# A state-space image block: the work between two batches' scans is rewritten (channels as 128 + 64, means summed on GpSimd, convolution in halves, a new order)

## The chip, the cores and the metric

The kernel runs on one core of a Trainium2 chip. The core has five engines, each with its own instruction queue: TensorE (PE, matrix products into PSUM), VectorE (DVE), ScalarE (ACT), GpSimd (POOL) and SyncE (SP, which here issues all DMAs). Engines meet only through semaphores. The metric is the device time of one launch in microseconds (us).

## The reference

The input x is 8 images of 64 x 64 positions with 192 channels, in float32. Two layers are applied, each as x + layer(groupnorm(x)). The change is in layer 1 (and in where layer 0's constants live), whose core is this:

```python
xz = jnp.einsum('bhwc,dc->bhwd', x, in_proj_w)          # 192 -> 768
xc, z = jnp.split(xz, 2, axis=-1)                       # 384 + 384 channels
xc = depthwise 3x3 convolution of xc; xc = silu(xc + conv_b)
xs = [rows, columns, rows reversed, columns reversed]   # K = 4 walks over 4096 positions
# per walk: x_dbl = x_proj(xs) -> dts, B, C;  delta = softplus(dt_proj(dts) + bias)
hst = exp(delta * A) * hst + (delta * u) * B            # 16 states a channel, 4096 steps
y   = sum over states of hst * C
y   = sum of the four walks (with + xs * Ds)
y   = layernorm(y) * ln_gamma + ln_beta
y   = y * silu(z)
out = einsum('bhwd,cd->bhwc', y, out_proj_w)            # 384 -> 192
```

## The kernel before

**Layer 0** works on all images first and leaves its result x1 in DRAM, channels outermost: 192 rows of 4,096 positions. Its means over channels use GpSimd adds (`s`, line 362) and one product with a matrix of ones.

**Layer 1** goes image by image ("batch" b). A batch has three parts:

- *front*: project x1 to the 384 channels of xc, fill a padded image, convolve, Silu, store to DRAM in row order and, turned, in column order (`xo`).
- *scan*: 32 steps (4 walks of 8 tiles), each with 24 units of states and channels. Per unit ScalarE makes the decays `ea`, PE turns the weighted inputs into `g`, VectorE runs `tensor_tensor_scan` (line 1596), GpSimd multiplies by C (`hc`, line 1610) and PE sums the states (`y`, line 1625). Results are added up in `yacc`, which stays in SBUF: 128 partitions x 3 groups of channels x 4,096 positions.
- *finish*: layer norm over the 384 channels of `yacc`, gate by silu(z), output projection, residual add, store.

The last loop of `layer1` runs for b = 0 to 8. In iteration b the finish of batch b-1 and the front of batch b are interleaved, together with the scan's prologue (the first chunk's loads, projections and weights); then the scan of batch b follows. So there are one front alone, seven boundaries (finish and front together) and one finish alone.

**How a boundary is ordered.** Front, finish and prologue are generators that yield `step(engine, weight, do)`, `"wait"` and `"take"` (a slot of a pool). `Flow` is a list planner: it keeps an estimated time per engine, picks the step that could start first (with `RANK` times the chain's rank as a bias), and fixes the instructions of each engine in that order. At run time every engine works through its list strictly in order. Weights, `LAG` and ranks only influence the order.

**The pieces.** Channels of x1 lie as 2 groups of 96 on 96 partitions (`CP, CT = 96, 2`). The front projects each tile of 512 positions with two products of 96 rows (`project`, line 1139), ScalarE copies the result into the pad (line 1169). When all eight tiles of a group of 128 channels are in, ScalarE does tap 0 (line 1190) and VectorE eight taps over 4,096 positions each (line 1200: `xs = pad * weight + xs`, three groups). Silu (line 1213) is done in halves, then a copy in turned order (line 1227) and the stores (1218, 1230). In the finish the mean is three products of `yacc` with a matrix of 1/384 (`mean`, line 1247), then VectorE subtracts (1255), ScalarE squares (1265), a second mean gives the variance, ScalarE makes 1/sqrt by Ln and Exp (1283, 1284), VectorE multiplies (1290), ScalarE applies gamma and beta (1297). The gate projects x1 again (1327), Silu (1345), VectorE multiplies (1357), PE projects back to 2 x 96 channels (1374), VectorE adds x1 (1383), SP stores (1386). The prologue loads `xc` and `wd` (1428, 1431), makes `p_d`, `xdbl`, `p_dt`, the softplus `spa`, `de`, `du` on GpSimd (1489), `duT`, and ten weightings `pw` (1554) before the first scan. In PSUM five banks (`mm`) serve all this, two the front's projection (`fx`), one the scan's prologue in steady state.

Of the kernel before, what the change touches and what calls it, by code (L numbers as in the profile page):

```python
# [16 lines left out]
CP, CT = 96, 2  # L17
# [73 lines left out]
class Flow:  # L91
# [48 lines left out]
    def start(self, req, ready):  # L140

        if req[0] == "wait":
            return (-1.0, max(ready, self.at[req[1]])) if req[1] in self.at else None
        if req[0] == "take":
            return (-1.0, max(ready, min(self.slots[req[1]]))) if self.slots[req[1]] else None
        engine, _, _, after, table = req
        t = max(ready if after is None else after, self.free[engine])
        if engine == "ACT" and table and table != self.table:
            return t + self.TABLE + self.STAY, t + self.TABLE
        return t, t  # L150

    def run(self):
        while self.chains:
# [8 lines left out]
            if req[0] == "take":  # L162
                self.slots[req[1]].remove(min(self.slots[req[1]]))
# [866 lines left out]
def layer1(tc, consts, x1s, mv1, out, w_in, w_x, w_dt, w_out):  # L1030
    nc = tc.nc
    ident, low, up, grp, eps, ones96, ones1, p96, p128 = consts
# [3 lines left out]
    image = lambda ap: ap.rearrange("(t p) l -> p t l", p=CP)  # L1036

    with ExitStack() as ctx:
# [8 lines left out]
        wi = wp.tile([CP, CT, 2 * DIN], F32, name="wi1")  # L1047
        nc.sync.dma_start(out=wi, in_=w_in.rearrange("(t p) m -> p t m", p=CP))
# [25 lines left out]
        sc, sh = gn_affine(tc, sp, mp, mv1.rearrange("p b t s -> p (b t) s"), grp, eps)  # L1074
        pb = mp.tile([128, TT], F32, name="p_gb", tag="mm")
        for m in range(2 * DT):
            for ct in range(CT):
                nc.tensor.matmul(
                    pb[:, m * nb : m * nb + nb],
                    wi[:, ct, m * 128 : m * 128 + 128],  # L1080
                    sh.rearrange("p (b t) -> p b t", t=CT)[:, :, ct],
                    start=ct == 0,
                    stop=ct == 1,
                )
# [3 lines left out]
        wxz = [wp.tile([CP, CT, DIN], F32, name=f"wi1{n}") for n in "xz"]  # L1088
# [4 lines left out]
        def scaled(f, b, half):  # L1093

            for ct in range(CT):
# [5 lines left out]
                            wxz[half][:, ct],  # L1101
                            wi[:, ct, half * DIN : half * DIN + DIN],
                            AF.Copy,
                            scale=sc[:, b * CT + ct : b * CT + ct + 1],
# [5 lines left out]
        def front(f, cx, mq, b, xo):  # L1110
# [3 lines left out]
            for tag, n in (("xl", 3), ("fx", 2), ("pad", 2), ("xs", 2), ("xt", 1)):  # L1114
                f.pool(tag, n)
            got = {}

            def load():
                for d in range(DT):
                    for t in range(NT):  # L1120
                        tk = slice(t * TT, t * TT + TT)
                        yield "take", "xl"
                        xl = got["xl", d, t] = fp.tile([CP, CT, TT], F32, name="xl1", bufs=3)
                        r = yield step("SP", 0.1, lambda: [nc.sync.dma_start(out=xl, in_=image(x1s[b])[:, :, tk])])
                        f.at["xl", d, t] = r + 3

            def project():
                yield from scaled(f, b, 0)
                for d in range(DT):
                    for t in range(NT):  # L1130
                        yield "wait", ("xl", d, t)
                        xl = got["xl", d, t]
                        yield "take", "fx"
                        ps = got["ps", d, t] = mq.tile([128, TT], F32, name="p_x1", tag="fx", bufs=2)
                        r = f.at["ps", d, t] = yield step(
                            "PE",
                            1.9,
                            lambda: [
                                nc.tensor.matmul(
                                    ps, wxz[0][:, ct, d * 128 : d * 128 + 128], xl[:, ct], start=ct == 0, stop=ct == 1  # L1140
                                )
                                for ct in range(CT)
                            ],
                        )
                        f.give("xl", r)

            def fill():
# [11 lines left out]
                for d in range(DT):  # L1159
# [18 lines left out]
                    f.at["pad", d] = r  # L1178

            def convolve():  # L1180
                for d in range(DT):
                    yield "wait", ("pad", d)
                    yield "take", "xs"
                    xs = got["xs", d] = fp.tile([128, HI, WI], F32, name="xs1", bufs=2)
                    tap = lambda j: pads[d % 2][:, j // 3 : j // 3 + HI, j % 3 : j % 3 + WI]
                    r = yield step(
                        "ACT",
                        3.7,
                        lambda: [
                            nc.scalar.activation(  # L1190
                                xs, tap(0), AF.Identity, bias=v["kb"][:, d : d + 1], scale=kw[:, d, 0:1]
                            )
                        ],
                    )
                    for j in range(1, 9):
                        r = yield step(
                            "DVE",
                            4.4,
                            lambda: [
                                nc.vector.scalar_tensor_tensor(xs, tap(j), kw[:, d, j : j + 1], xs, ALU.mult, ALU.add)  # L1200
                            ],
                            r - f.LAG,
                        )
                    f.give("pad", r)
                    f.at["conv", d] = r

            def store():
                for d in range(DT):
                    yield "wait", ("conv", d)
                    xs = got["xs", d]  # L1210
                    for h in range(2):
                        half = xs[:, h * HI // 2 : h * HI // 2 + HI // 2]
                        r = yield step("ACT", 1.9, lambda: [nc.scalar.activation(half, half, AF.Silu)], None, "silu")
                        r = yield step(
# [5 lines left out]
                                    in_=half.rearrange("p h w -> p (h w)"),  # L1220
                                )
                            ],
                            r,
                        )
                    yield "take", "xt"
                    xt = fp.tile([128, WI, HI], F32, name="xt1")
                    r = yield step("ACT", 7.2, lambda: [nc.scalar.copy(xt, xs.rearrange("p h w -> p w h"))])
                    f.give("xs", r + 5)
# [4 lines left out]
                f.at["front"] = r  # L1233

            return [convolve(), fill(), project(), load(), store()]

        def finish(f, cx, mq, b):
# [3 lines left out]
            for tag, n in (("sq", 1), ("rs", 2), ("z", 2), ("xl2", 3)):  # L1241
# [4 lines left out]
            def mean(ps, src):  # L1246
                return [nc.tensor.matmul(ps, on, src[:, d], start=d == 0, stop=d == DT - 1) for d in range(DT)]

            def centre():
                for t in range(NT):  # L1250
                    yv = yacc[:, :, tk(t)]
                    yield "take", "mm"
                    pm = mq.tile([128, TT], F32, name="p_m", tag="mm")
                    q = yield step("PE", 2.8, lambda: mean(pm, yv), 0.0)
# [4 lines left out]
            def square():  # L1259
                for t in range(NT):  # L1260
# [5 lines left out]
                    yield "take", "mm"  # L1266
                    pv = got["pv", t] = mq.tile([128, TT], F32, name="p_v", tag="mm")
                    r = yield step("PE", 2.8, lambda: mean(pv, sq))
# [39 lines left out]
            def load():  # L1308
                for t in range(NT):
                    yield "take", "xl2"  # L1310
                    xl = got["xl2", t] = fp.tile([CP, CT, TT], F32, name="xl2", bufs=3)
                    r = yield step("SP", 0.1, lambda: [nc.sync.dma_start(out=xl, in_=image(x1s[b])[:, :, tk(t)])])
                    f.at["xl2", t] = r + 3

            def gate():
                yield from scaled(f, b, 1)
                for t in range(NT):
                    yield "wait", ("xl2", t)
                    xl = got["xl2", t]
                    for d in range(DT):  # L1320
                        yield "take", "mm"
                        ps = got["pz", t, d] = mq.tile([128, TT], F32, name="p_z1", tag="mm")
                        f.at["pz", t, d] = yield step(
                            "PE",
                            1.9,
                            lambda: [
                                nc.tensor.matmul(
                                    ps, wxz[1][:, ct, d * 128 : d * 128 + 128], xl[:, ct], start=ct == 0, stop=ct == 1
                                )
                                for ct in range(CT)  # L1330
                            ],
                            f.at["xl2", t],
                        )

            def silu():
                for t in range(NT):
                    yield "take", "z"
                    z = got["z", t] = fp.tile(full, F32, name="z", bufs=2)
                    for d in range(DT):
                        yield "wait", ("pz", t, d)  # L1340
                        ps = got["pz", t, d]
                        p = yield step(
                            "ACT",
                            0.6,
                            lambda: [nc.scalar.activation(z[:, d], ps, AF.Silu, bias=gb[:, DT + d, b : b + 1])],
                            None,
                            "silu",
# [507 lines left out]
```

## Time and profile before

| what | us |
|---|---|
| three runs: lowest, median, highest | 24181.09, 24186.39, 24191.97 |
| the profiled execution: its time | 24176.65 |
| the profiled execution: span from the first to the last instruction | 24174.9 |
| layer 0 and first front, up to the first scan | 5049.5 |
| one batch, scan to scan | 2,404 |
| of that: between the last scan of a batch and the first of the next | 237.8 to 240.1 |
| last scan to the end | 137.0 |

Times in the profile count from the first instruction's start. A row of a group gives line, engine, operation, tiles (output <- inputs), shape and count; then busy time and mean duration in ns; then the idle time of the engine just ahead of these instructions and what ended it. A row of the timeline has start, duration (several merged instructions: from the first's start to the last's end), engine, line, operation, tiles and count. "PEld" is the load of weights into PE; each float32 product shows as two passes. A row of a stretch has the busy time and count of each engine, then PE's granted clock, the busy share of the DMA engines and GB/s.

### The profile page before, as it was taken

How to read it: one execution, taken by the hardware profiler on the slowest of the kernel's cores; microseconds unless marked ns; L12 is line 12 of the kernel's file. 1: busy time of each engine (PE TensorE's matmuls, PEld its weight loads, DVE VectorE, ACT ScalarE, POOL GpSimd, SP SyncE). 2: the span in 40 equal slices, each digit the busy share in tenths (PEclk: the TensorE clock that was granted, in tenths of full speed). 3: DMA queues.
4: the chain of work that ended last, by engine and by line, in shares of the span. 5: the costliest groups of instructions: out<-in, count | busy, mean ns of one | idle time of the engine just before them, and what ended most of it. 6: DMA issues, size and time to landing. Idle time of an engine off the chain costs nothing.

```text
span 24174.9 us, 313055 instructions
## 1 busy us (share of the span) xinstructions
PE 20986.5 (87%) x100036; PEld 10182.8 (42%) x100036; DVE 21386.3 (88%) x22093; ACT 21415.5 (89%) x38076; POOL 16907.4 (70%) x13639
## 2 busy tenths in 40 slices
PE   7999999978888888888888888888888888888888
PEld 4444444434443444344434443444344434443444
DVE  7888888779998998899889988998899989998998
ACT  5666766679998999899989998999899989998998
POOL 1111111159986998699869986998699779977997
PEclk8999999989999999999999999999999999999999
DMA  2111111122222222222222222222222222222222
GB/s 49 44 44 44 49 44 42 36 86 67 68 66 87 68 67 68 89 66 66 69 87 68 68 68 86 67 68 70 84 68 67 76 78 67 68 75 82 67 67 58
DMA packets 1129702, 1608.05 MB, mean 67 GB/s; under 512 B 259360, under 2 KB 458432, under 8 KB 1118848
## 3 DMA queue, kind: packets, MB, share of 16 engines
q1 hardware_dynamic: 1128064, 1588.03, 23.4%
q8 instruction: 806, 13.21, 0.2%
q14 instruction: 832, 6.82, 0.1%
HBM read 1024.65 MB, written 160.17 MB: 49 GB/s over the span
## 4 chain that ended last, share of the span: by engine, by line
POOL 53%; PE 25%; issue 8%; DVE 6%; ACT 5%; DMA 2%; SPq 1%; POOLq 0%; DVEq 0%; ACTq 0%
POOL hc L1610 47%; POOL cy L1608 4%; PE y L1625 3%; PE p_f L953 3%; DVE xs L1200 3%; PE p_f L973 2%; PE p_x L445 2%; PE g L1580 2%; ACT pw L1554 2%; DMA xc<-xo 2%; PE p_o L870 1%; POOL du L1489 1%; ACT ea L1569 1%; PE p_y L787 1%; PE p_d L1439 1%
## 5 line engine op out<-in xcount | busy, mean ns | idle before, releaser
L1610 POOL TENSOR_TENSOR hc<-hs,cb 128x1024 f32<-128x1024 f32 x6144 | 14577.7, 2373 | 10.3 <-POOL cy L1608 6.7
L1596 DVE TENSOR_TENSOR_SCAN hs<-ea,cy,g 128x512 f32<-128x512 f32 x10752 | 13069.7, 1263 | 783.2 <-PE g L1580 468.3
L1554 ACT ACTIVATE pw<-duT,bt 128x384 f32<-128x384 f32 x16384 | 8875.8, 601 | 11.6 <-DVE duT L1502 11.6
L1625 PE MATMUL y<-hc,sel 128*64 128x512 f32 x24576 | 6658.3, 620 | 2229.1 <-POOL hc L1610 2221.3
L1569 ACT ACTIVATE ea<-dr,an 128x512 f32<-128x512 f32 x12288 | 8123.2, 709 | 159.9 <-DVE hs L1596 131.9
L1580 PEld LDWEIGHTS g<-ident,pw 128*128 128x128 f32 x49152 | 5309.6, 141 | 4320.1 <-issue 2676.5
L1580 PE MATMUL g<-ident,pw 128*128 128x128 f32 x49152 | 6793.2, 280 | 32.4 <-DVE hs L1596 12.9
L1625 PEld LDWEIGHTS y<-hc,sel 128*64 128x64 f32 x24576 | 1229.6, 135 | 3648.1 <-POOL hc L1610 3385.1
L1489 POOL TENSOR_TENSOR du<-de,xc 128x512 f32<-128x512 f32 x768 | 982.9, 1280 | 1632.9 <-DVE de L1482 1618.2
L1608 POOL COPY cy<-hs 128x2 f32<-128x2 f32 x6144 | 1161.7, 189 | 1324.4 <-DVE hs L1596 1211.9
L1596 DVE TENSOR_TENSOR_SCAN hs<-ea,g 128x512 f32<-128x512 f32 x1536 | 1777.0, 1204 | 178.7 <-PE g L1580 138.3
L362 POOL TENSOR_TENSOR s<-xs 96x512 f32<-96x512 f32 x64 | 121.0, 1891 | 2033.2 <-DVE xs L340 1522.3
L1200 DVE SCALAR_TENSOR_TENSOR xs<-pad,p,xs 128x4096 f32<-128x4096 f32 x192 | 860.8, 4484 | 37.6 <-ACT xs L1190 30.4
L1468 PE MATMUL p_dt<-xdbl,wd 13*128 13x512 f32 x1536 | 856.8, 639 | 41.7 <-DVE de L1482 39.7
L362 POOL TENSOR_TENSOR s<-sq 96x512 f32<-96x512 f32 x128 | 210.3, 1643 | 961.7 <-ACT sq L375 890.7
L1439 PE MATMUL p_d<-xc,wx 128*44 128x512 f32 x1536 | 792.2, 598 | 95.0 <-DMA xc<-xo 95.0
L340 DVE SCALAR_TENSOR_TENSOR x<-xx,p,x 96x512 f32<-96x512 f32 x1024 | 784.4, 814 | 19.4 <-ACT x L329 19.4
L953 PE MATMUL p_f<-h,wf 96*128 96x512 f32 x1536 | 764.1, 633 | 24.4 <-ACT zs L547 14.0
L340 DVE SCALAR_TENSOR_TENSOR xs<-xin,p,xs 96x512 f32<-96x512 f32 x1024 | 749.5, 768 | 4.6 <-ACT xs L329 4.6
L1482 DVE SCALAR_TENSOR_TENSOR de<-p_dt,spa 128x512 f32<-128x512 f32 x768 | 524.1, 682 | 254.0 <-ACT spa L1477 253.0
L973 PE MATMUL p_f<-m,wf 128*96 128x512 f32 x1536 | 693.3, 602 | 0.0
L1495 PEld LDWEIGHTS p_du<-ident,du 128*128 128x128 f32 x3072 | 323.1, 141 | 743.2 <-POOL du L1489 500.3
(201 smaller groups left out, 19729.0 us busy)
## 6 DMA issues: line engine op xcount, KB each, us to landing
cb<-cd SPq DMA_DIRECT2D x4096, 128.0 KB
dr<-de SPq DMA_DIRECT2D x3072, 128.0 KB
xc<-xo SPq DMA_DIRECT2D x256, 768.0 KB
e<-csd SPq DMA_DIRECT2D x256, 384.0 KB
xl<-x SPq DMA_DIRECT2D x256, 384.0 KB
xo<-xs SPq DMA_DIRECT2D x48, 1024.0 KB
xo<-xt SPq DMA_DIRECT2D x24, 2048.0 KB
xl<-in_x SPq DMA_DIRECT2D x64, 384.0 KB
```

The costliest lines, as they stand in the source:

```text
L340: nc.vector.scalar_tensor_tensor(im(out[:, ct]), tap(ct, j), w[:, ct, j : j + 1], im(out[:, ct]), ALU.mult, ALU.add)
L953: nc.tensor.matmul(ps, wf1[:, ct, mt * 128 : mt * 128 + 128], h[:, ct], start=ct == 0, stop=ct == 1)
L973: nc.tensor.matmul(ps[:CP], wf2[:, kt, ct * CP : ct * CP + CP], m[:, kt], start=kt == 0, stop=kt == 5)
L1200: nc.vector.scalar_tensor_tensor(xs, tap(j), kw[:, d, j : j + 1], xs, ALU.mult, ALU.add)
L1489: o(nc.gpsimd.tensor_mul(st["du", d], st["de", d], st["xc"][:, d]))
L1554: nc.scalar.activation(st["pw", p, j][:, :, i], st["duT"][:, j].rearrange("p (g c) -> p g c", c=64), AF.Copy, scale=st["bt"][:, j, n : n + 1],
L1569: nc.scalar.activation(ea[:, f], state[s]["dr", d][:, f], AF.Exp, scale=an[:, k, p, at : at + 1])
L1580: nc.tensor.transpose(g[:, f, j * 128 : j * 128 + 128], state[s]["pw", p, j][:, 2 * d + f].rearrange("p a b -> p (a b)"), ident,)
L1596: nc.vector.tensor_tensor_scan(rev(h[:, f]), rev(ea[:, f]), rev(g[:, f]), 0.0 if first(s) else state[s - 1]["cy"][:, p, d, f : f + 1], ALU ...
L1608: o(nc.gpsimd.tensor_copy(st["cy"][:, p, d], h[:, :, last]))
L1610: o(nc.gpsimd.tensor_mul(hc, h, bc(st["cb", p], 1, [128, 2, TT])))
L1625: o(nc.tensor.matmul(y[half[f]], sel, hc[:, f], start=p == 0 and k > 0, stop=p == NP1 - 1))
```

## The change

In layer 1's front and finish only; the scan's code is the same.

- **Channels as 128 + 64.** x1, `wi` and the scaled weights lie as 128 channels on 128 partitions, and the other 64 of two neighbouring tiles side by side: tile t on partitions 0 to 63, tile t+1 on 64 to 127 (`parts`). A pair of tiles is loaded by three DMAs and projected by four products (`pair`): two of 128 rows, and two of 64 rows on different halves of the array. The output projection makes 128 channels per tile and the 64 of both tiles side by side in one PSUM tile; residual adds go from four of 96 partitions a pair to three of 128. The group norm's scale and shift go through DRAM once to lie the same way (`affd`, `aff`).
- **Means** first add the three channel groups on GpSimd (two adds of 128 x 512), then one product.
- **Convolution in halves** of 32 rows: tap 0 and the taps of a half start when its part of the pad is filled, Silu, store and turned copy follow by halves.
- **Order anew**: every chain has a rank, `RANK` is 1.0, `LAG` 0.35, new weights; `take` can ask for two slots; means and gate of tiles from 4 on are planned behind the last convolution's first half (`LATE`); the prologue may be planned as soon as the last store in row order is due. PSUM: `mm` has three banks, the gate two of its own (`zz`).
- Constants used by layer 0 alone are released after it, `wd` has one buffer.

```diff
+            free, n = sorted(self.slots[req[1]]), req[2] if len(req) > 2 else 1
+            return (-1.0, max(ready, free[n - 1])) if len(free) >= n else None
...
+    def parts(ap, xl, t):
+        two = ap.rearrange("c (t l) -> c t l", l=TT)[:, t : t + 2]
+        return [(xl[:, 0:2], two[0:128])] + [(xl[i * 64 : i * 64 + 64, 2], two[128:C, i]) for i in range(2)]
+
+    def pair(w, m, ps, xl):
+        out = [nc.tensor.matmul(ps[i], w[:, 0, m], xl[:, i], start=True, stop=False) for i in range(2)]
+        for i in range(2):
+            rows = slice(i * 64, i * 64 + 64)
+            out.append(nc.tensor.matmul(ps[i], w[rows, 1, m], xl[rows, 2], start=False, stop=True))
+        return out
...
+        for i, a in enumerate((sc, sh)):
+            for ct in range(CT):
+                nc.sync.dma_start(
+                    out=affd[ct * CP : ct * CP + CP, i], in_=a.rearrange("p (b t) -> p t b", t=CT)[:, ct]
+                )
+        nc.sync.dma_start(out=aff[:, 0], in_=affd[0:128])
+        for i in range(2):
+            nc.sync.dma_start(out=aff[i * 64 : i * 64 + 64, 1], in_=affd[128:C])
...
             def convolve():
                 for d in range(DT):
-                    yield "wait", ("pad", d)
...
+                    for h in range(2):
+                        yield "wait", ("pad", d, h)
+                        yield "take", "xs"
+                        xs = got["xs", d, h] = fp.tile([128, HI // 2, WI], F32, name="xs1", bufs=4)
+                        at = h * HI // 2
+                        tap = lambda j: pads[d % 2][:, at + j // 3 : at + j // 3 + HI // 2, j % 3 : j % 3 + WI]
...
-            return [convolve(), fill(), project(), load(), store()]
+            return [(convolve(), 0.04), (fill(), -0.2), (project(), -0.11), (load(), -0.38), (store(), 0.29)]
+        LATE = {4: 0}
...
-            def mean(ps, src):
-                return [nc.tensor.matmul(ps, on, src[:, d], start=d == 0, stop=d == DT - 1) for d in range(DT)]
+            def mean(src):
+                yield "take", "ys"
+                ys = fp.tile([128, TT], F32, name="ys", bufs=2)
+                yield step(
+                    "POOL",
+                    2.6,
+                    lambda: [nc.gpsimd.tensor_add(ys, src[:, 0], src[:, 1]), nc.gpsimd.tensor_add(ys, ys, src[:, 2])],
+                )
+                yield "take", "mm"
+                ps = mq.tile([128, TT], F32, name="p_m", tag="mm")
+                r = yield step("PE", 1.0, lambda: [nc.tensor.matmul(ps, on, ys, start=True, stop=True)])
...
-                        st["wd"] = pools["pr1"].tile([45, DIN], F32, name="wd")
+                        st["wd"] = pools["pr1"].tile([45, DIN], F32, name="wd", bufs=1)
...
-            f.STAY = 0.0
+            f.LAG, f.STAY, f.RANK = 0.35, 0, 1.0
...
-            mq = mq_x.enter_context(tc.tile_pool(name="mq1", bufs=5, space=PSUM, reuse_waits="tile"))
-            f.pool("mm", 5)
+            mq = mq_x.enter_context(tc.tile_pool(name="mq1", bufs=3, space=PSUM, reuse_waits="tile"))
+            f.pool("mm", 3)
```

## The prediction

> **What bounds the kernel now.** I read the page first (engine shares and the chain that ended last), then the stretches between the scans engine by engine, the groups of one such boundary, and its timeline.
>
> ```profile
> PE 20986.5 (87%) x100036; PEld 10182.8 (42%) x100036; DVE 21386.3 (88%) x22093; ACT 21415.5 (89%) x38076; POOL 16907.4 (70%) x13639
> POOL 53%; PE 25%; issue 8%; DVE 6%; ACT 5%; DMA 2%; SPq 1%; POOLq 0%; DVEq 0%; ACTq 0%
> ...
> 4867.00:5049.00 182.00, 72.46 (x157) 30.95 (x158) 112.68 (x34) 74.33 (x60) 4.67 (x7) 0.65 0.44 144
> 7217.00:7456.00 239.00, 192.18 (x427) 76.89 (x428) 166.30 (x76) 140.86 (x144) 7.45 (x10) 0.91 0.41 128
> 24038.00:24175.00 137.00, 127.75 (x296) 52.78 (x296) 54.91 (x43) 64.09 (x79) 2.76 (x3) 0.98 0.17 46
> ```
> Shares of the whole hide the stages: 53% of the chain is GpSimd, nearly all of it hc in the eight scans, which the change leaves alone. It touches the first front (row two of the stretches: 182 us), seven boundaries like the third row (239 us; columns are PE, PEld, DVE, ACT, POOL busy, clock, DMA share, GB/s) and the last finish (137 us): nearly 2,000 us in all. In a boundary PE is busy 192 of 239 and DVE 166, while POOL does 7.
>
> ```profile
> 7211.12 5.94 DVE L1596 TENSOR_TENSOR_SCAN hs<-ea,cy,g 128x512 f32<-128x512 f32 x5
> 7265.16 9.09 DVE L1200 SCALAR_TENSOR_TENSOR xs<-pad,p,xs 128x4096 f32<-128x4096 f32 x2 [1.14 <-ACT xs L1190]
> 7375.11 9.01 DVE L1200 SCALAR_TENSOR_TENSOR xs<-pad,p,xs 128x4096 f32<-128x4096 f32 x2
> 7456.46 4.55 DVE L1596 TENSOR_TENSOR_SCAN hs<-ea,g 128x512 f32<-128x512 f32 x4 [1.31 <-PE g L1580]
> ...
> L1200 DVE SCALAR_TENSOR_TENSOR xs<-pad,p,xs 128x4096 f32<-128x4096 f32 x24 | 107.6, 4484 | 2.0 <-ACT xs L1190 1.1
> L1255 DVE TENSOR_TENSOR yacc<-yacc,p_m 128x1536 f32<-128x1536 f32 x8 | 14.0, 1753 | 27.8 <-PE p_m L1247 27.8
> L1383 DVE TENSOR_TENSOR xl<-p_o,xl 96x512 f32<-96x512 f32 x16 | 10.8, 683 | 12.4 <-PE p_o L1374 12.4
> ```
> So the boundary has three stretches on DVE. A: last scan to first convolution tap, 7217.1 to 7265.2, 48.1 us, paced by PE, which alternates projection and means. B: the 24 taps, to 7384.1, 119.0 us, DVE full. C: last tap to first scan, 72.3 us, a latency chain with PE's leftovers of the finish in it.
>
> **The change by parts.** PE's unit is a pass: the six of one mean start 2.58 us ahead of the next group, 0.43 each; a full product is two.
>
> ```profile
> 7229.41 2.74 PE L1247 MATMUL p_v<-ysq,on 128*128 128x512 f32 x6
> 7231.99 1.88 PE L1139 MATMUL p_x<-xl,wi1x 96*128 96x512 f32 x4
> ```
> *PE.* A mean falls from 6 passes to 2: 16 x 4 x 0.43 = 27.5 us less. A pair of tiles falls from 8 passes to 4 full and 4 half-array ones. No row here shows 64 rows beside 64 rows; the nearest, two 64-column products (y, L1625), start 0.01 us apart, so I take 2.6 us a pair; ends 2.6 and 3.44 (no overlap). 24 pairs save 20 us, the output product 4 x 2.4 = 10. PE falls by 57 us and is not the bound any more.
>
> The Trainium skill (TensorEngine Tiling (Array Packing), Key Properties) says that tiles work independently but that a change of tiling mode drains the array. By its first half a pair is 2.6, by its second somewhat more; nothing here measures that.
>
> *DVE.* Half a tap: L340 (512 elements) takes 0.739 and L1200 (4,096) 4.484, so 1.045 ns an element and 0.20 fixed: 2.34, with the 0.045 gap of the present chain 2.39. 48 are 114.7 against 108.7 (ends 2.26 and 2.45). Residual adds go from 16 to 12: -2.7.
>
> *GpSimd, and the price of it.* Each mean brings two adds of 128x512; du (L1489), of the same shape, takes 1.27, so 16 x 2.54 = 41 us on an engine that is idle here. But:
>
> ```profile
> 4098.07 6.94 POOL L362 TENSOR_TENSOR s<-xs 96x512 f32<-96x512 f32 x1 [38.54 <-DVE xs L340]
> 4097.85 6.04 DVE L340 SCALAR_TENSOR_TENSOR x<-xx,p,x 96x512 f32<-96x512 f32 x9
> 4103.82 1.24 DVE L604 TENSOR_TENSOR w<-dt,dec 128x24 f32<-128x24 f32 x1
> 7430.00 1.27 POOL L1489 TENSOR_TENSOR du<-de,xc 128x512 f32<-128x512 f32 x1 [0.49 <-DVE de L1482]
> 7430.48 2.40 DVE L1290 TENSOR_TENSOR yacc<-yacc,yrs 128x1536 f32<-128x1536 f32 x1
> ```
> A GpSimd add that takes 1.26 elsewhere took 6.94 behind nine DVE operations with two SBUF inputs, the form of the taps; and a DVE product of 1.75 took 2.40 when du had started 0.48 us before it. They exclude each other, both ways. After its own end a tap leaves a gap of 0.045, in which a waiting add gets in; then the next tap waits for it, about 0.96 by these rows (2.40 - 1.75 = 0.65, plus the 0.48 by which du was ahead, less the overlap of 0.1 and the gap). The second add of the mean waits for that tap, and takes another 0.96.
>
> The Trainium skill (SBUF — State Buffer, Who interferes with whom) says the same: a DVE instruction with two SBUF inputs and a GpSimd one that reads SBUF hold the shared port exclusively, and the loser waits for the whole instruction. By it a meeting costs DVE up to 1.27, so 18 meetings 23 us where the rows give 17.
>
> *Stretch A becomes 29.* The first tap needs five tiles of the pad, not eight: three pair loads of x, with two of z ahead of the third in SP's queue. The first is out early; the other four follow what is 5.0 us after the scan at 786 KB each. The DMA gave 260 GB/s at share 1.06 (7225 to 7229), so 3.0 each: 5.0 + 1.6 to land (cd<-xdbl to cb<-cd) + 12.1 = 18.7. Then a pair 2.6, fill 0.7, ACT's square and gate work ahead of it 3, tap 0 on ACT 2.0, hand-overs 1.5: 28.5.
>
> *Stretch B becomes 164.* Taps 114.7; by the new order 15 products and subtractions of 1.75 stand among them, 26.3, and six adds, 4.1; waits for means 2. Of the 28 GpSimd adds in it I count 18 that begin under a tap or a two-input product, the rest under subtractions, adds or DVE's waits: 18 x 0.96 = 17. Ends: 0, and 28 x 1.0 = 28.
>
> *Stretch C becomes 46.* Last tap to issue of the turned copy: table 1.3, Silu of a half 1.9, one scaling 0.8, half a copy 3.7, hand-overs 0.5: 8.2 (now 12.6). From there to p_d 11.8 as now (7396.7 to 7408.5; same bytes, SP still sends xc behind xt). From p_d to the first scan now 48.0, with p_o and p_v between p_d's products; the new order keeps these three together, and the first front, which has no finish in it, shows 25.9:
>
> ```profile
> 5023.61 5.11 PE L1439 MATMUL p_d<-xc,wx 128*44 128x512 f32 x6 [69.89 <-DMA xc<-xo]
> 5049.48 3.44 DVE L1596 TENSOR_TENSOR_SCAN hs<-ea,g 128x512 f32<-128x512 f32 x3 [5.85 <-ACT ea L1569]
> ...
> 7408.46 1.91 PE L1439 MATMUL p_d<-xc,wx 128*44 128x512 f32 x2 [4.06 <-DMA xc<-xo]
> ```
> One gate pair and an output product that remain cost what the cold PE costs there (p_d 5.1, warm 2.6).
>
> The boundary: 29 + 164 + 46 = 239 against 239.4. The 19 us won in A and 26 in C go to B (+45): 22 because finish work and its waits move into it, 6 for halving the taps, 17 to the exclusion. Seven: -3.
>
> *Last finish.* PE 127.8 of 137 now. After: eight tiles of the norm chain at some 8 us each on ACT (square 1.5, Ln and Exp 1.3, three scalings 2.4, waits) 64; then 62 less 7.8 of early gate work for four pairs (3 x 2.6 and 7.8 of output), 55; lead 5, larger last store 1.5: 125.5, -11.5 (ends -17 and -6).
>
> *First front.* The affine now goes through DRAM: four stores behind gn_nb and three loads, some 0.3 each to issue, 1.6 to land each way and many 4-byte pieces: +7 (ends +4, +14) ahead of p_gb, whose 5.3 us nothing covers. The halves win and lose about equally there.
>
> *Costed at nothing.* Loads and stores go from 40 DMAs a boundary to 60; at 0.35 to issue that is 7 us more of SP, under gaps of 4 us between its loads now; in C three stores of out stand among the twelve dr transfers, about 1 us if dr is what ea waits for. GpSimd's du stands behind the last sum, which ends some 30 us before it is due; a sum that is late comes off C directly. The wait of tiles 4 to 7 on the convolution's tail orders the plan and adds no semaphore. wd with one buffer is reloaded a scan step (some 67 us) after its last reader; if it did wait, SP would hold back cb and dr, a few us in each of 24 places. Layer 0's instructions keep their order.
>
> Sum: -3 - 11.5 + 7 = -7.5. The profiled execution took 24,176.7 (span 24,174.9), 9.7 below the median of the three runs; against that median 24,179.
>
> **Rivals.** *The exclusion costs little:* adds slip under subtractions and waits. For it: the median s<-sq add takes 1.284, hardly delayed. Against it: DVE is full in B. Without the 17: 24,179 - 119 = 24,060. *Slower: late means stall DVE.* A mean met twice takes 1.2 + 1.27 + 2.3 + 1.27 = 6.0, not 2.5. Five subtractions stand among the taps in DVE's fixed order, and every tap behind one waits for its mean. For it: subtractions wait 27.8 us for p_m already. Against: sums are issued early for some. It decides once it adds 7 us a boundary, two of the five without slack beyond my count; three give 10, so 24,249. *Half-array products don't overlap:* 0.84 a pair on five pairs of A, one of C and the end, about 5 each: 24,214.
>
> **How the numbers follow.** The measurement can tell about 0.2%, 48 us. The forecast 0.38 (own range 24,138 to 24,235), little exclusion 0.27, stalls 0.29, serial products 0.06. That gives faster 0.27, same 0.44, slower 0.29. The range takes in both unknown ends of the exclusion: 24,060 to 24,270.
>
> **What would show it.** Right: first tap 27 to 33 us after the scan; half taps 2.34; DVE gaps of about 1 us between taps where adds run, and adds on GpSimd of 3 us and more in the mean; p_d within 21 us of the last tap; PE below 140 busy in a boundary. Wrong: adds of 1.27 throughout under the taps, boundaries below 230 or above 247, or a scan period other than now.

## The result

The changed kernel takes 24,164.65 us (median of 12 runs, 24,149.9 to 24,178.4), the kernel before 24,188.57 (12 runs, 24,173.4 to 24,198.2): a ratio of 0.9991, 95% interval 0.9982 to 0.9999. That is 24 us less, 0.1%, and half of the 48 us that the prediction named as the least it could tell from nothing. The forecast was 24,179, its range 24,060 to 24,270.

The profiled execution has a span of 24,162.9 us against 24,174.9, so it shows 12.0 of the 24. The first two lines are from the page (busy time by engine, and the chain that ended last).

```profile
PE 20682.9 (86%) x99524; PEld 9992.5 (41%) x99524; DVE 21520.2 (89%) x22253; ACT 21455.3 (89%) x38157; POOL 17442.6 (72%) x13895
POOL 53%; PE 23%; issue 8%; DVE 8%; ACT 5%; DMA 2%; SPq 1%; POOLq 0%; DVEq 0%; ACTq 0%
```

DVE is 134 us busier although it executes no more arithmetic on the taps, and GpSimd is 535 us busier. The stretches answer to the three rows shown of before: first front, one boundary, last finish (columns: PE, PEld, DVE, ACT, POOL busy, clock, DMA share, GB/s).

```profile
4874.90:5071.50 196.60, 64.34 (x159) 25.83 (x160) 117.78 (x58) 76.24 (x69) 4.42 (x6) 0.62 0.44 136
7239.00:7471.00 232.00, 154.89 (x372) 53.81 (x372) 184.81 (x96) 141.40 (x147) 75.34 (x42) 0.81 0.41 134
24030.00:24163.00 133.00, 98.32 (x232) 32.14 (x232) 53.52 (x39) 60.37 (x77) 50.19 (x35) 0.87 0.16 48
```

In the boundary PE fell from 192 to 155 and DVE rose from 166 to 185. DVE's timeline gives the ends of the three stretches: the last scan, the first tap, the last taps, the next scan.

```profile
7231.64 7.13 DVE L1670 TENSOR_TENSOR_SCAN hs<-ea,cy,g 128x512 f32<-128x512 f32 x6 [0.59 <-POOL cy L1682]
...
7266.37 2.61 DVE L1226 SCALAR_TENSOR_TENSOR xs<-pad,p,xs 128x2048 f32<-128x2048 f32 x1 [0.47 <-ACT xs L1214]
...
7422.78 4.74 DVE L1226 SCALAR_TENSOR_TENSOR xs<-pad,p,xs 128x2048 f32<-128x2048 f32 x2
...
7470.74 3.44 DVE L1670 TENSOR_TENSOR_SCAN hs<-ea,g 128x512 f32<-128x512 f32 x3 [3.17 <-PE g L1654]
```

Over the seven boundaries the stretches are in the mean A 28.0 (before 47.7), B 161.2 (119.4) and C 42.5 (71.6), together 231.8 against 238.7. Not all of these 6.9 us are won: 3 go back within the first 8 of the 24 units of the scan's first step. ScalarE is behind there: it loads a function table (1.28 us) 1.8 us after the first scan, where before it did so 8.3 us ahead of it, and then still has weightings `pw` to make. PE's `g` waits for them, and DVE's seventh scan waits 2.7 to 3.4 us for `g`, where it was 0.5. A boundary measured past the first step (from the end of the last hc of one batch to the end of the 32nd of the next; a step has 24) is 325.6 against 329.5: 3.9 us less, 27 in all. Between those marks the scans take 2,072 to 2,075 us in both kernels. This longer measure, "to step one", is used below.

The whole account of the profiled executions, after minus before: the first front +13.4 (from the end of the last gn_ps product to the first scan 196.6, before 183.2), seven boundaries -27.2, the last finish -3.9, the scans -3.0, and layer 0 +8.6. The last can't be told from chance: the end of the last gn_ps product lies anywhere between 4,858.6 and 4,885.8 us in the ten profiled executions below and these two, although those ten have the layer 0 of the changed kernel, instruction by instruction. Without it the account is -21, near the 24 of the medians.

### The profile page after: what moved, and what is told of

Same layout as the page of the kernel before. It is cut to its first block, busy times and chain, and to the rows that moved or that the text cites. A ratio compares the mean times of both kernels' runs of the same rounds, so it can differ in the third digit from the quotient of the medians.

```text
span 24162.9 us, 312700 instructions
## 1 busy us (share of the span) xinstructions
PE 20682.9 (86%) x99524; PEld 9992.5 (41%) x99524; DVE 21520.2 (89%) x22253; ACT 21455.3 (89%) x38157; POOL 17442.6 (72%) x13895
## 4 chain that ended last, share of the span: by engine, by line
POOL 53%; PE 23%; issue 8%; DVE 8%; ACT 5%; DMA 2%; SPq 1%; POOLq 0%; DVEq 0%; ACTq 0%
POOL hc L1684 47%; POOL cy L1682 4%; DVE xs L1226 3%; PE y L1699 3%; PE p_f L954 3%; PE p_f L974 2%; PE p_x L446 2%; ACT pw L1628 2%; ACT ea L1643 2%; DMA xc<-xo 2%; PE g L1654 2%; POOL du L1563 2%; PE p_o L871 1%; PE p_y L788 1%; PE p_z L529 1%
## 5 line engine op out<-in xcount | busy, mean ns | idle before, releaser
L1226 DVE SCALAR_TENSOR_TENSOR xs<-pad,p,xs 128x2048 f32<-128x2048 f32 x384 | 997.5, 2599 | 29.1 <-ACT xs L1214 18.8
L341 DVE SCALAR_TENSOR_TENSOR x<-xx,p,x 96x512 f32<-96x512 f32 x1024 | 784.3, 814 | 19.4 <-ACT x L330 19.4
## 6 DMA issues: line engine op xcount, KB each, us to landing
cb<-cd SPq DMA_DIRECT2D x4096, 128.0 KB
dr<-de SPq DMA_DIRECT2D x3072, 128.0 KB
xl<-x SPq DMA_DIRECT2D x256, 128.0 KB
```

The lines of the kernel that those rows point to most:

```text
L341: nc.vector.scalar_tensor_tensor(im(out[:, ct]), tap(ct, j), w[:, ct, j : j + 1], im(out[:, ct]), ALU.mult, ALU.add)
```

## Experiments

All are timed beside runs of the kernel before (medians 24,186, 24,184 and 24,189 in the three groups); the differences below are to the changed kernel's 24,165 unless another is named. The table has what their profiled executions show, in us: the mean of seven boundaries for A, B, C and "to step one", then the mean of a tap, the first front and the last finish.

| kernel | A | B | C | to step one | tap | front | finish | median |
|---|---|---|---|---|---|---|---|---|
| before | 47.7 | 119.4 | 71.6 | 329.5 | 4.484 | 183.2 | 137.0 | 24,188.6 |
| changed | 28.0 | 161.2 | 42.5 | 325.6 | 2.634 | 196.6 | 133.0 | 24,164.7 |
| no sums | 27.7 | 144.8 | 42.7 | 308.6 | 2.350 | 199.3 | 124.8 | 24,027.9 |
| means on PE | 31.5 | 153.2 | 41.9 | 320.2 | 2.350 | 199.3 | 133.4 | 24,117.7 |
| one input | 28.6 | 148.8 | 42.9 | 313.5 | 2.412 | 199.2 | 123.6 | 24,066.0 (one run) |
| affine by PE | 28.1 | 161.0 | 42.5 | 325.5 | 2.634 | 180.6 | 135.6 | 24,141.0 |
| same rows | 31.5 | 164.0 | 42.7 | 332.1 | 2.631 | 200.6 | 139.2 | 24,225.7 |
| before, with sums | 46.8 | 123.3 | 72.6 | 333.6 | 4.631 | 183.3 | 147.4 | 24,215.7 |
| whole taps | 35.1 | 128.8 | 89.1 | 343.7 | 4.683 | 210.4 | 133.2 | 24,304.9 |
| no late wait | 28.5 | 159.2 | 59.4 | 337.8 | 2.602 | 199.2 | 134.8 | 24,253.6 |
| hybrid | 28.0 | 149.6 | 41.4 | 312.7 | 2.356 | 180.6 | 132.7 | 24,056.4 |
| hybrid, replanned | 28.3 | 143.5 | 60.1 | 322.6 | 2.356 | 180.3 | 128.0 | 24,125.7 |

### The sums left out: the whole of their price

My theory was the prediction's: the sums take the port from DVE. The rival was that a half tap is slow for another reason.

```diff
-  POOL: tensor_add(ys, src[:, 0], src[:, 1]); tensor_add(ys, ys, src[:, 2])
-  PE:   matmul(ps, on, ys)
+  PE:   matmul(ps, on, src[:, 0])
```

> The changed kernel with the sums left out: a mean is one product of the first third of its channels (the mean over 128 of the 384 channels, so that part of the computation is left out). No GpSimd work and no more PE work than in the changed kernel, the order the same: the whole price of the sums. Theory 1 (exclusion and the sums' own latency): half taps 2.34, boundary 232 to 212, last finish some 5 shorter, time near 24,020. Theory 2 (half taps are slower by nature beside ACT, PE or the DMAs): taps stay at 2.6, boundary 228 or more, time above 24,130.

Measured: 24,027.9 (ratio to before 0.9935, interval 0.9919 to 0.9950). The taps, the products and the subtraction, by group between 5,200 and 24,000 us, first in the changed kernel, then without the sums (instructions, then busy us and mean ns, then idle time before them). The kernel without sums is early enough that some instructions of its last finish fall into this stretch (64 and 62 where seven boundaries have 56); the means can be compared, the totals of those lines can't:

```profile
L1226 DVE SCALAR_TENSOR_TENSOR xs<-pad,p,xs 128x2048 f32<-128x2048 f32 x336 | 885.1, 2634 | 11.9 <-ACT xs L1214 3.3
L1335 DVE TENSOR_TENSOR yacc<-yacc,yrs 128x1536 f32<-128x1536 f32 x56 | 120.3, 2148 | 0.0
L1404 DVE TENSOR_TENSOR yacc<-yacc,z 128x1536 f32<-128x1536 f32 x56 | 103.8, 1884 | 1.1 <-ACT z L1391 0.2
L1302 DVE TENSOR_TENSOR yacc<-yacc,p_m 128x1536 f32<-128x1536 f32 x56 | 97.9, 1749 | 129.5 <-PE p_m L1292 129.5
```

```profile
L1226 DVE SCALAR_TENSOR_TENSOR xs<-pad,p,xs 128x2048 f32<-128x2048 f32 x336 | 789.7, 2350 | 13.0 <-ACT xs L1214 2.8 <-DMA xl<-x 0.5
...
L1335 DVE TENSOR_TENSOR yacc<-yacc,yrs 128x1536 f32<-128x1536 f32 x64 | 112.2, 1752 | 9.1 <-ACT yrs L1329 9.1
L1404 DVE TENSOR_TENSOR yacc<-yacc,z 128x1536 f32<-128x1536 f32 x62 | 106.8, 1753 | 15.7 <-ACT z L1391 13.7 <-ACT yacc L1342 1.0
```

So the sums made a tap 0.284 us longer in the mean, and the products, which have two SBUF inputs too, 0.396 (with yrs) and 0.131 (with z). The subtraction, which takes p_m from PSUM, stays at 1.749. A boundary has 48, 8 and 8 of these: 13.6 + 3.2 + 1.0 = 17.8 us. "To step one" fell by 17.0. The price of the sums in a boundary is the exclusion and hardly anything else. Instruction by instruction, 16 taps and 4 products a boundary are the delayed ones, 0.89 us each. A timeline of both engines in the changed kernel shows how:

```profile
7293.16 3.19 POOL L1288 TENSOR_TENSOR ys<-ys,yacc 128x512 f32<-128x512 f32 x1
7295.15 2.81 DVE L1335 TENSOR_TENSOR yacc<-yacc,yrs 128x1536 f32<-128x1536 f32 x1
7296.31 2.78 POOL L1288 TENSOR_TENSOR ys<-yacc 128x512 f32<-128x512 f32 x1
7297.89 2.82 DVE L1404 TENSOR_TENSOR yacc<-yacc,z 128x1536 f32<-128x1536 f32 x1
7299.17 2.67 POOL L1288 TENSOR_TENSOR ys<-ys,yacc 128x512 f32<-128x512 f32 x1
7300.63 3.35 DVE L1226 SCALAR_TENSOR_TENSOR xs<-pad,p,xs 128x2048 f32<-128x2048 f32 x1
```

Each product of 1.75 lasts 2.8 and each add of 1.27 lasts 2.7 to 3.2: they take turns, and the wait lies inside the record, with no gap between the instructions. An add waits for one tap at most: none of the 154 in B lasts over 3.32 us. The add of 6.94 us that the prediction shows from layer 0 waited for nine; there each tap's record overlaps the next by 0.07 us, while without sums a tap starts 0.035 us (median) after the end of the one before. The last finish fell too, from 133.0 to 124.8. There are no taps there: DVE's waits for p_m fell by 6.0 us, since each mean had waited for two adds, and the products with yrs became 2.2 us shorter in all.

### Means back on PE

```diff
-  POOL: tensor_add(ys, src[:, 0], src[:, 1]); tensor_add(ys, ys, src[:, 2])
-  PE:   matmul(ps, on, ys)
+  PE:   matmul(ps, on, src[:, d]) for d in range(3)
```

> The changed kernel with every mean back on PE as three products and no sums on GpSimd; the order on every engine is that of the changed kernel. Theory 1 (the sums cost DVE by exclusion): half taps fall from 2.63 us in the mean to 2.34, the product by yrs from 2.15 to 1.75, stretch B from 161 to 143; PE takes 27 us more a boundary, most of it in its gaps in B, about 3 in A. Boundary 232 to 216, last finish 3 to 8 longer; time some 105 below the changed kernel, near 24,060. Theory 2 (the means paid for the boundary by relieving PE): PE binds again, taps are 2.34 but DVE waits for p_m between them, boundary 232 or longer, time 24,165 or above.

Measured: 24,117.7 (ratio 0.9973, 0.9962 to 0.9983), 47 below the changed kernel, where 105 were expected. Theory 1 holds for the taps (2.350); theory 2 has a part of the truth. The boundary came to 226.7, not 216, since DVE now waits for means. The line of the subtraction in the same stretch (58 of them, two from the last finish):

```profile
L1302 DVE TENSOR_TENSOR yacc<-yacc,p_m 128x1536 f32<-128x1536 f32 x58 | 101.7, 1753 | 211.0 <-PE p_m L1292 211.0
L1335 DVE TENSOR_TENSOR yacc<-yacc,yrs 128x1536 f32<-128x1536 f32 x56 | 98.2, 1753 | 23.5 <-ACT yrs L1329 23.4
```

In the seven boundaries alone the wait for p_m rose from 129.5 to 203.1, 10.5 a boundary, and the wait for yrs by 3.3 a boundary: of the 17.8 that the exclusion gives back, all but 5.4 "to step one" go to a PE that has three products to do where the order has room for one. In this order, then, three products on PE cost 11.6 us a boundary "to step one" and the sums 17.0.

### One input instead of two

```diff
-  POOL: tensor_add(ys, src[:, 0], src[:, 1]); tensor_add(ys, ys, src[:, 2])
+  POOL: tensor_copy(ys, src[:, 0]); tensor_copy(ys, src[:, 2])
```

> The changed kernel with the two adds of each sum replaced by two copies of 128x512 on GpSimd, each with one SBUF input (the mean is then that of the last third alone, so that part is left out); the same places in the order. Theory 1 (whatever GpSimd reads from SBUF excludes DVE): half taps stay near 2.6 and the copies last 2 us and more in the mean, boundary 228 to 233. Theory 2 (only GpSimd's operations with two inputs exclude): half taps 2.34, copies at their own time throughout, boundary 212 to 218.

```profile
L1288 POOL COPY ys<-yacc x128: 606/613/2667, 7238.1 to 23988.4; 128x512 f32<-128x512 f32 x128
L1288 POOL COPY ys<-ysq x128: 613/1157/2736, 7248.7 to 23997.7; 128x512 f32<-128x512 f32 x128
```

One run alone, 24,066.0. The numbers are the shortest, the median and the longest, in ns. A copy with one SBUF input is shut out too: 0.61 us alone, up to 2.74 behind a tap. So one SBUF input on GpSimd's side is enough (a copy also writes SBUF, and no run separates the two), and theory 2 is wrong; but theory 1's taps of 2.6 did not come either. A copy is short, and it takes less from DVE: 15 delayed instructions a boundary at 0.28 us, 4.2 in all, against 20 at 0.89. The boundary came to 220.3, 5.1 above that without sums. What an exclusion costs DVE follows the length of the GpSimd instruction, but not in proportion: in both kernels it is that length (0.61, 1.27) less 0.33 to 0.38 us.

### The affine by PE

```diff
-  affd[...] = sc, sh (four stores to DRAM); aff[:, 0], aff[0:64, 1], aff[64:128, 1] = affd (three loads)
+  PE:  p_aff = slices of ident x (sc, sh), 16 small products
+  DVE: aff = p_aff
```

> The changed kernel with the affine turned to 128 + 64 rows by products with slices of the identity on PE and one copy on DVE, in place of the four stores to DRAM and three loads. Theory 1 (the round trip stands on the path of the first front): PE's wait ahead of p_gb falls from 19.4 us to about 3, the first scan comes 16 earlier, time 24,149. Theory 2 (the loads of wi or x are what is late there, the trip runs beside them): the wait becomes one for a load, the first scan comes less than 5 earlier.

The changed kernel's timeline of the trip, then that of the kernel with the affine by PE:

```profile
4875.46 0.91 SPq L1096 DMA_DIRECT2D affd<-gn_sc  x2
4876.47 2.09 SPq L1096 DMA_DIRECT2D affd<-gn_nb  x2
...
4891.90 0.34 SPq L1099 DMA_DIRECT2D aff<-affd  x1
4892.29 1.10 SPq L1101 DMA_DIRECT2D aff<-affd  x2
4893.43 3.46 SPq L1148 DMA_DIRECT2D xl<-x  x6
...
4894.30 5.80 PE L1105 MATMUL p_gb<-aff,wi 128*128 128x8 f32 x22 [19.42 <-issue]
```

```profile
4886.44 1.00 PE L1096 MATMUL p_aff<-gn_sc,ident 96*96 96x8 f32 x8 [0.61 <-ACT gn_sc L85]
...
4888.44 0.19 DVE L1103 COPY aff<-p_aff 128x32 f32<-128x32 f32 x1 [1.84 <-PE p_aff L1096]
...
4888.68 6.35 PE L1107 MATMUL p_gb<-aff,wi 128*128 128x8 f32 x24 [0.29 <-DVE aff L1103]
```

Theory 1 holds: the last store is issued by 4,878.6 and the first load only at 4,891.9, 13.3 us later, and the loads of x stand in SP's queue behind it. PE waits 19.4 us; without the trip, p_gb starts 2.8 after gn_ps. The first front is 180.6 against 196.6 (199 in four other kernels with the trip), so the trip costs 16 to 19 us, and the rest of the change shortens the front by 2.6. The median is 24,141.0 (0.9984, 0.9976 to 0.9993), 24 below the changed kernel.

### Half-array products on the same rows

```diff
-  rows = slice(i * 64, i * 64 + 64)
+  rows = slice(0, 64)
```

> The changed kernel with both half-array products of a pair on rows 0 to 63 (so the second tile of a pair takes the 64 channels of the first: that part is computed on other data); instructions, loads and order are the same. Theory 1 (side by side they overlap, on the same rows they do not): the four half passes of a pair take 1.7 us instead of 1.1, A grows by 4, the boundary by 4 to 6, time 24,165 plus 28 to 42. Theory 2 (PE has gaps enough everywhere): the half passes are slower, the boundary within 1.5 us of 232.

PE's timeline of one pair and what follows it, in the changed kernel and on the same rows:

```profile
7253.21 1.98 PE L1046 MATMUL p_x<-xl,wi1x 128*128 128x512 f32 x4
7255.12 1.13 PE L1049 MATMUL p_x<-xl,wi1x 64*128 64x512 f32 x4
7256.18 1.12 PE L1292 MATMUL p_m<-ys,on 128*128 128x512 f32 x2
```

```profile
7250.69 1.98 PE L1046 MATMUL p_x<-xl,wi1x 128*128 128x512 f32 x4
7252.61 1.98 PE L1049 MATMUL p_x<-xl,wi1x 64*128 64x512 f32 x4
7254.52 1.13 PE L1292 MATMUL p_m<-ys,on 128*128 128x512 f32 x2
```

The four half passes take 1.06 us from start to start (7255.12 to 7256.18), on the same rows 1.91. So they do run side by side; their starts lie 0.006 us apart. Theory 1 holds, above its sizes: A grew by 3.5, "to step one" by 6.5, the last finish by 6.2, and the time to 24,225.7 (1.0018, 1.0008 to 1.0027), 61 more where 28 to 42 were expected.

### The sums alone, in the kernel before

```diff
-  PE:   matmul(ps, on, src[:, d]) for d in range(3)
+  POOL: tensor_add(ys, src[:, 0], src[:, 1]); tensor_add(ys, ys, src[:, 2])
+  PE:   matmul(ps, on, ys)
```

> The kernel before with one part of the change alone: a mean is the sum of its three tiles by two GpSimd adds and one product on PE. Layout, whole taps and plan are those of before; each pair of adds stands where the three products stood (to make room, the constants of layer 0 are let go after it and wd has one buffer, as in the changed kernel). Theory 1 (the sums pay where PE binds and cost where DVE is full): twelve of sixteen means lie in stretch A or its first taps, where PE binds, few under later taps; A falls from 48 to about 40, B grows by some 4, C falls by 4, the last finish by 10; boundary 230, time near 24,110. Theory 2 (PE stands in its fixed order behind each sum, two adds late): A stays at 48 or grows, boundary 240 or more, time 24,180 or above.

Measured: 24,215.7 (1.0014, 1.0005 to 1.0023), some 26 above before. I had expected 24,110. A was 46.8, hardly below 47.7, where it should have fallen to 40. The timeline there:

```profile
7243.68 1.12 PE L1251 MATMUL p_v<-ys,on 128*128 128x512 f32 x2 [0.94 <-POOL ys L1250]
...
7244.18 2.28 DVE L1295 TENSOR_TENSOR yacc<-yacc,yrs 128x1536 f32<-128x1536 f32 x1 [1.37 <-ACT yrs L1289]
7244.93 2.66 POOL L1250 TENSOR_TENSOR ys<-ys,yacc 128x512 f32<-128x512 f32 x1
...
7247.64 1.12 PE L1251 MATMUL p_m<-ys,on 128*128 128x512 f32 x2 [1.12 <-POOL ys L1250]
...
7251.44 1.12 PE L1251 MATMUL p_v<-ys,on 128*128 128x512 f32 x2 [0.95 <-POOL ys L1250]
```

All three waits of PE are for ys. From p_v to p_v it is 7.76 us; in the kernel before, where PE had no such wait, it was 8.59, from the p_v at 7229.41 that the prediction shows to this one:

```profile
7238.00 2.74 PE L1247 MATMUL p_v<-ysq,on 128*128 128x512 f32 x6
```

Two sums, one of which meets the product with yrs (2.28 and 2.66 us), and the square between them are the chain now. B grew by 3.9, most of it by taps of 4.631, and the last finish by 10.4. So in that kernel the sums gain 0.9 us a boundary in A and cost 3.9 in B and 1.0 in C: they do not pay. This is theory 2, though not by PE's order alone: GpSimd is what PE waits for.

### Whole taps, and the late wait

```diff
-  for h in range(2): ... 8 taps of (128, HI // 2, WI)
+  8 taps of (128, HI, WI), behind ("pad", d, 1)
```

> The changed kernel with the convolution whole again: 24 taps of 4,096 a boundary, the first behind all eight tiles of the pad; Silu, store and turned copy stay in halves, behind the last whole tap. Theory 1 (the halves pay at the ends of B): A 28 to about 38, B some 6 shorter by the fixed part of 24 taps, C 43 to about 48; boundary 232 to 240, time near 24,225. Theory 2 (the halves give nothing, since the plan has other work for DVE at both ends): boundary within 3 us of 232, time within 25 of 24,165.

Measured: 24,304.9 (1.0049, 1.0036 to 1.0063), 80 us beyond theory 1. B fell by 32, more than the fixed part of 24 taps; C grew by 47. The planner now puts fewer of the finish's steps between the taps (8 adds lie in B, not 22), and the rest stands in C. So this shows what halves and plan give together. What the halves alone are worth stays open; their fixed part can be read without it: 48 taps of 2.350 are 5.2 us more than 24 of 4.484.

```diff
-  LATE = {4: 0}
+  LATE = {}
```

> The changed kernel without the wait of tiles 4 to 7 of the finish for the tail of the convolution; all else is left to the planner. Theory 1 (that wait only orders the plan, and the same work stands under the taps either way): boundary within 3 us of 232, time within 25 of 24,165. Theory 2 (without it finish work is put ahead of the first taps): A grows by 8 or more, C falls by less, boundary 236 or more, time above 24,190.

Measured: 24,253.6 (1.0029, 1.0018 to 1.0040), 89 above the changed kernel: neither theory. A is the same (28.5) and B 2 shorter, but C is 59.4, not 42.5. PE's timeline in C:

```profile
7450.23 4.72 PE L1513 MATMUL p_d<-xc,wx 128*44 128x512 f32 x6 [7.43 <-DMA xc<-xo]
...
7460.64 3.42 PE L1046 MATMUL p_z<-xl,wi1z 128*128 128x512 f32 x4
...
7482.31 5.46 PE L1420 MATMUL p_o<-yacc,wo 128*128 128x512 f32 x6 [3.15 <-DVE yacc L1404]
7487.70 3.10 PE L1433 MATMUL p_o<-yacc,wo 128*64 128x512 f32 x12
7491.69 1.94 PE L1654 MATMUL g<-ident,pw 128*128 128x128 f32 x16 [0.89 <-DVE xl L1446]
```

Pairs of p_z and two output products stand between p_d and g, the first product that the scan needs; from p_d to the first scan it is 38.1 to 42.7 us here and 25.8 to 27.5 in the changed kernel. That one wait in the plan is worth 12 us a boundary, "to step one".

### A version that takes both findings

```diff
   affine by PE, as above
-  mean(src): sum on GpSimd for all
+  mean(src): sum on GpSimd for the means of tiles 0 to 3; three products on PE for the rest
```

> The changed kernel with the affine by PE, and with sums on GpSimd only where no taps run: the means of tiles 0 to 3 and the variance of tile 0 in a boundary, and all of the last finish; the other eleven means of a boundary are three products on PE. The order on every engine is that of the changed kernel. Theory 1 (price of a sum by place): A 28 as with sums, taps 2.36, DVE's waits for p_m some 8 a boundary as with all means on PE; boundary 222, first front as with the affine by PE; time near 24,065. Theory 2 (what the exclusion cost comes back as waits for PE in B): boundary 227 or more, time above 24,095.

One correction: in the last finish this kernel sums the means on GpSimd but leaves the variances to PE, and in a boundary the variance of tile 0 is summed as the expectation says.

Measured: 24,056.4 (0.9946, 0.9934 to 0.9959), 108 us below the changed kernel and 128 below the runs of before beside it: the best of all that keep the computation.

```profile
L1228 DVE SCALAR_TENSOR_TENSOR xs<-pad,p,xs 128x2048 f32<-128x2048 f32 x336 | 791.4, 2355 | 11.9 <-DMA xl<-x 2.3 <-ACT xs L1216 0.9
```

A is that of the sums (28.0), the taps are at 2.355, and B is 4.8 us longer than without the sums. Of the 108 us, 90 come from the boundaries (12.9 each) and 16 from the first front.

The last kernel tells the planner the true times of these means.

> The hybrid, with the planner told the true times of its means (2.8 on PE for three products, no GpSimd step for them), so that the order around them is made anew. Theory 1: DVE's waits for p_m in B (some 4 us a boundary in the hybrid) go, boundary 216, time 24,030 to 24,056. Theory 2 (the ranks fit the old costs): some finish work falls behind the last tap, C grows, boundary 222 or more, time above 24,070.

Measured: 24,125.7 (0.9976, 0.9967 to 0.9986), 69 above the hybrid. It is theory 2 in full: the boundary is 231.9, B fell to 143.5, C rose to 60.1. The planner fills B better and has put finish work into the chain of C, as without the late wait. Only the last finish gained, to 128.0.

## Why the prediction was right, and where not

**The forecast held for the reason given.** A fell by 19.7 (19 forecast), C by 29.1 (26), and B grew by 41.8 (45). The exclusion, the term that decided between the forecast and its first rival, was priced at 18 meetings of 0.96, 17 us a boundary; it measured 20 of 0.89, 17.8. With the sums out the kernel takes 24,028, where the rival "the exclusion costs little" gave 24,060. That rival is dead. What made up A's fall is shown in part: A grows by 3.5 with the means back on PE, by 3.5 with the half-array products in turn, and by 7.1 with whole taps and the plan that they bring; the rest of the 19.7 no run takes apart.

**That the total came so near is partly luck.** The profiled account without layer 0 is -21 where the sum had -7.5. The boundaries gave 24 us more than the sum said and the scans 3 more; the last finish gave 7.6 less and the first front cost 6.4 more. These errors have opposite signs.

**The sign of its appearance was wrong.** I looked for gaps of 1 us on DVE and for adds of 3 us and more in the mean. The wait lies inside the tap's record (2.337 at the shortest, 3.358 at the longest), and the adds in B take 2.5 in the mean: only the second add of a variance's sum comes to 3.19 in the median. The product of 2.40 us that I quoted from before had shown where the wait lies.

**Stretch C, and with it the boundary.** 46 was forecast and 42.5 came, p_d 15.8 us after the last tap where I had 20. But I ended the boundary at the first scan. In the long measure 3 of the 7 us a boundary went back. The row was there: before's first batch, whose front has no finish in it, takes 2,167.6 us from its first to its last scan, the others 2,164. The step that failed is "from p_d to the first scan": the first scan is not what the scan's pace hangs on, since ScalarE's weightings are not done by then.

**PE.** The term "PE falls by 57 us" measured 37 (192 to 155), and the bound of 140 that I gave for it was passed. A pair is 2.94 us, not 2.6: the half passes take 1.06, not 0.86, and the first pass after a change between full and half comes 0.52 after the one before, not 0.43. A mean of two passes is 1.0, not 0.86. These account for half of the 20 us. The rest may go with the granted clock, 0.81 in the boundary where it was 0.91; no run separates that. PE is not the bound, so none of this shows in the boundary. The Trainium skill (TensorEngine Tiling (Array Packing), Key Properties) says that tiles work independently and that a change of mode drains the array. Starts 0.006 us apart agree with the first half; the 0.1 us a change would be the second, but no run here shows that a drain is its cause.

**The last finish: -3.9, not -11.5.** The step that failed counted eight tiles of the norm chain by ACT and left out that each mean now waits for two adds. Without the sums it is 124.8, near the 125.5 of the step. By the long way on PE it is 133.4, so there the sums gain nothing and lose nothing.

**The first front: +13.4, not +7 (ends +4 and +14).** The mis-sized term is the trip through DRAM: 16 to 19 us, of which 13.3 lie between the last store's issue and the first load's. I had 1.6 to land each way, from a DMA of larger pieces, and added too little for the many small ones: 5.8 of the 13.3 us went by while their packets still moved, and in the other 7.5 nothing moved. The front's other parts gained 2.6, where I had them even.

**The rivals.** Late means did not stall DVE: of 18.5 us a boundary that the subtractions wait for p_m, 17.1 lie ahead of the first tap and 1.4 in B. Put back on PE, the means brought more of it, 10.5 us a boundary, 6.2 of them in B. The rival "half-array products do not overlap" was priced at 24,214; when it was made true the time was 24,226.

**Costed at nothing, and worth much: the order.** I took the order as given and asked only what stands on the path in it. Two changes of the plan that move no work cost 12 us (no late wait) and 10 us (replanned, against the hybrid) a boundary, "to step one", each more than twice the 3.9 that the whole change gained there.

The Trainium skill (SBUF — State Buffer, Who interferes with whom) says that a DVE instruction with two SBUF inputs contends with a GpSimd one that reads SBUF and that the loser waits for the whole of it. The runs agree on who meets: adds and one-input copies both, with taps and products, and not with the subtraction that reads PSUM (1.749 us with adds, 1.752 without). The price that they show is less than the whole instruction: 0.89 us a meeting with an add of 1.27, 0.28 with a copy of 0.61.

## What to carry to other kernels

An idle GpSimd is not free beside a DVE that is full of operations with two SBUF inputs: count the meetings, price each by the length of the GpSimd instruction (here less some 0.35 us), and put such work where DVE waits anyhow, as the hybrid does in stretch A. Measure a stage to the point where the next one runs at its own pace, not to its first instruction. And where a plan orders the work, the order is itself a term of the sum: a change of costs or waits in it can move more than the work that was saved.

## What the runs showed of the hardware that I had not expected

- A one-input copy on GpSimd is held back by DVE as an add is (0.61 us alone, up to 2.74), but costs DVE only 0.28 us a meeting.
- Half passes side by side start 0.006 us apart, four take 1.06 us where four in a row take 1.91, and each change between full and half costs some 0.1 us.
- The stores of the affine are 12 KB, moved in over 3,000 packets of 4 bytes. The last packet had moved by 4,884.4 us, and for the 7.5 us from there to the first load the DMA engines moved nothing. SP's waits in the changed kernel put the 13.1 us ahead of the first load down to the last store; what passes between its last packet and its signal the profile does not show.

```profile
SPq L1099 <- DMA affd<-gn_nb: 13.1, 1, 13.1
```

- Layer 0, with its instructions in the same order, ended anywhere in a stretch of 27 us, as much as the whole difference between the two kernels. The granted clock over it goes nearly in step: 0.924 in the mean where it ended first (4,858.6), 0.920 at 4,870.4 and 4,874.9, 0.917 where it ended last (4,885.8).
